# A two-layer decoder on one core: the first layer's pairs, its experts and the preparation of the second layer's weights planned as one graph, constants loaded inside it, expert weights laid out contiguously

## The chip, the core and the metric

The kernel runs on one core of a Trainium2 chip, as one launch of one program. The metric is the device time of that program in microseconds (us). Times are medians over several runs. A profile is one further execution, recorded instruction by instruction. The engines are TensorE (PE, with its weight loads PEld), VectorE (DVE), ScalarE (ACT), GpSimd (POOL) and SyncE (SP). SP and ACT issue ordinary DMAs, POOL issues indirect ones.

## What is computed

The input `x` has 32 sequences of 100 tokens with 256 channels, and there is a context of 361 rows for each sequence. Everything is 32-bit float. Two post-norm layers run one after the other:

```
x = layernorm(x + L0_attn(x))        # 16 heads of 16, rotary, causal
x = layernorm(x + L0_xattn(x, ctx))  # 8 heads, strided context positions
x = layernorm(x + L0_ffn(x))         # 64 experts of width 176, best 6 for each token, at most 128 tokens
                                     # to an expert, and one shared expert of width 352
x = layernorm(x + L1_attn(x))        # linear attention
x = layernorm(x + L1_xattn(x, ctx))  # full softmax over 361 rows, gated output
x = layernorm(x + L1_ffn(x))         # weights rounded to -1, 0, 1, activations to 8 bits
```

What matters here: an expert cannot start until every token of every sequence has chosen its experts, because the list of an expert's tokens runs over all of them; and the second layer's feed-forward needs both of its weight matrices reduced to a mean absolute value and then rounded (the "ternary weights").

## The kernel before

The program has four stages, one after the other.

1. **Start** (L434 to L553). The three down-projections of the first attention (1 MB each) are loaded by SP and multiplied on PE with their up-projections (L439 to L456). Then SP loads all constants of the first layer (L457 to L479: `wc`, `wqx`, `wkx`, `wvx`, `wox`, biases, `ws13`, `ws2`, rotary tables, masks). ACT's queue meanwhile writes zeros into the six routing tables (L515), into the tail of `x_dram` and `y_dram[0]` and, in 26 DMAs of 128 KB, into all of `y_dram[1]` (L521), and then loads every constant of the second layer (L527 to L548).
2. **Pairs** (`pair`, L608). The sequences go through the first layer two at a time, 16 pairs. A pair loads `xT`, `x` and its context `cR` (736 KB, two buffers), projects, sends queries and keys through DRAM (`dd`) into padded tiles `qpad` and `kpad`, does two score passes with a maximum between them (`nmx`, `nmT`, written into `qpad` by small DMAs), sends the result through DRAM again (`odd`, `sgd`), then cross attention from `cR` (keys at L781, values at L849), routing on DVE, and 12 indirect DMAs on POOL that write each token and its weight into the routing tables (L966). The shared expert's result goes to `y_dram[0]` (L1004).
3. **Experts** (`slots` L1008, `expert` L1038). `slots` reads the six tables into `lists` (L1014), adds them up (L1018), turns the result (L1024) and makes the row numbers `sidx` (L1029 to L1033). Then for each of 64 experts: SP loads `w13` (352 KB, as 256 rows of 1408 bytes) and `w2e` (176 KB, as 176 rows of 1024 bytes); POOL gathers 128 rows of `x_dram` (`xe`, L1046); PE turns them (L1054), multiplies by `w13` (through `dense`, L384) and by `w2e` (L1084); ACT and DVE do the gate; POOL scatters the result with an add into one of two `y_dram` (L1090). The weights have 6 buffers each, `xe`, `xeT` and `he` 3, `ye` 4. `prepare` (L555) has the same graph with the lowest priority: it makes `wog` and `bog` for the second layer from `wout` and `wgateT`, and the ternary weights `w1q` and `w2q` out of 1 MB loads into `wf` (L584 to L604).
4. **Second layer** (`sequence`, L1123): 32 sequences, one at a time in the program but overlapped by the planner.

The order of the work inside stages 2, 3 and 4 is set by a planner, `Flow` (L89 to L235). Every operation is entered with its engine, a cost in us, a latency for DMAs, what it reads and writes, and a priority. `emit` (L174) then steps through a clock of its own and picks, engine by engine, the operation that could start first, and among those the one with the lowest priority times `step` less the longest chain behind it. Buffers are rings with a fixed order of use; an operation that has no free buffer waits. The planner knows no DMA bandwidth: a DMA has a fixed latency whatever else is under way. What it decides is a fixed order for each engine, and on the chip each engine runs its list in that order, waiting where an input is late. Stages 2 and 3 have a graph each (`step` 20 and 1.5), with a pool of SBUF buffers each (`wa`, `we`). In the built program the DMAs of SP and ACT take eight completion semaphores in turn, and a DMA is not issued before the one that last had its semaphore has landed.

Of the kernel before, what the change touches and what calls it, by code (L numbers as in the profile page):

```python
# [238 lines left out]
def tile_decoder(ctx: ExitStack, tc: tile.TileContext, d, out):  # L239
# [56 lines left out]
    class Kit:  # L296
# [7 lines left out]
        def op(self, eng, cost, fn, r=(), w=(), **k):  # L304
            return self.fl.op(eng, cost, fn, r, w, pri=self.pri, **k)
# [151 lines left out]
    wc0 = w2(cA, "wc")  # L457
    wqx, wkx, wvx, wox = (w2(cA, n) for n in ("wqx", "wkx", "wvx", "wox"))
    bqx, bkx, bvx = (col(cA, n) for n in ("bqx", "bkx", "bvx"))
    nc.vector.tensor_scalar(bqx, bqx, SC32, None, ALU.mult)  # L460
    box = brow(cA, "box", T)
    gwT, gb = w2(cA, "gwT"), brow(cA, "gate_b", T, E)
    ws13 = w2(cA, "ws13")
    ws2 = cA.tile([128, 3, D], F32, name="ws2")
    nc.vector.memset(ws2[96:128, 2, :], 0.0)
    nc.sync.dma_start(ws2[:, 0:2, :], d["ws2T"][0:256].rearrange("(i p) n -> p i n", p=128))
    nc.sync.dma_start(ws2[0:96, 2, :], d["ws2T"][256:SI])

    nc.vector.tensor_scalar(ws2, ws2, 0.5, None, ALU.mult)
    rot0 = [table(cA, n) for n in ("cose", "sine", "coso", "sino")]  # L470
    pairmask, spread2 = table(cA, "pairmask"), table(cA, "spread2")
    causal = [table(cA, n) for n in ("causal", "causalT")]
# [3 lines left out]
    for i, t in enumerate(causal):  # L476
        mb = cA.tile([T, 4, T], BF16, name=f"mask{i}")
        nc.vector.tensor_copy(mb, t.unsqueeze(1).broadcast_to([T, 4, T]))
        masks.append(mb.rearrange("p r t -> p (r t)"))  # L479


    bvl_ = cA.tile([128, KC, T], F32, name="bvl_")
    for k in range(KC):
        nc.vector.tensor_scalar(bvl_[:, k, :], ones[:, 0:T], bvx[:, k : k + 1], None, ALU.mult)
    p = bank("pb")
    dense(p[0:T, 0:D], bvl_, wox)
    nc.vector.tensor_tensor(box, p[0:T, 0:D], box, ALU.add)
# [32 lines left out]
    for i in range((NTOK + CAP) // 128):  # L520
        nc.scalar.dma_start(y_dram[1][i * 128 : (i + 1) * 128, :], zero)  # L521
# [4 lines left out]
    q2 = nc.scalar  # L526
    wqkl, wvl, wol = (w2(cB, n, q2) for n in ("wqkT", "wvT", "woT"))  # L527
    bqkl, bvl, bol = brow(cB, "bqk", T, 2 * D, q2), brow(cB, "bv", T, D, q2), brow(cB, "bo", T, D, q2)
    headmask, spread = table(cB, "headmask", q2), table(cB, "spread", q2)
    wq1, wk1, wv1 = (w2(cB, n, q2) for n in ("wq1", "wk1", "wv1"))  # L530
    gam, bet = col(cB, "gamma", q2), col(cB, "beta", q2)
    cosq1, sinq1, cosk1, sink1, ebias = (
        table(cB, n, q2) for n in ("cosq1", "sinq1", "cosk1", "sink1", "ebias"))
    n1w, n2w = brow(cB, "norm1_w", T, D, q2), brow(cB, "norm2_w", T, HID, q2)
    asc, abi = brow(cB, "act_scale", T, 1, q2), brow(cB, "act_bias", T, 1, q2)
# [7 lines left out]
    q2.dma_start(wog[:, :, 0:D], d["woutT"].rearrange("(k p) n -> p k n", p=128))  # L543
    bog = cB.tile([T, 2 * D], F32, name="bog")
    for o, nm in enumerate(("bout", "bgate")):
        q2.dma_start(
            bog[:, o * D : (o + 1) * D],
            d[nm].rearrange("(o n) -> o n", o=1).broadcast_to([T, D]))  # L548

# [5 lines left out]
    def prepare(k):  # L555

        wraw, wg = k.V("wraw", [128, KC, D], 1), k.V("wg", [128, KC, D], 1)
        bcol, bl = k.V("bcol", [128, KC], 1), k.V("bl", [128, KC, T], 1)
# [12 lines left out]
        for m in range(KC):  # L571
# [8 lines left out]
            bog[:, D : 2 * D], bog[:, D : 2 * D], p[0:T, 0:D], ALU.add), r=[p])  # L580
        n = KC * HID
        for i, (nm, dst, nk) in enumerate((("w1fT", w1q, KC), ("w2fT", w2q, HID // 128))):
            wf, s, p = k.V("wf", [128, n], 1), k.V("ws", [128, 2]), k.P1()
            k.op("SP", 0.3, lambda wf=wf, nm=nm, nk=nk: nc.sync.dma_start(  # L584
                wf.t.rearrange("p (k n) -> p k n", k=nk),
                d[nm].rearrange("(k p) n -> p k n", p=128)), w=[wf], lat=6.0)
            k.op("DVE", 2.3, lambda wf=wf, s=s: nc.vector.tensor_reduce(
                s[:, 0:1], wf.t, AX.X, ALU.add, apply_absolute_value=True), r=[wf], w=[s])
            k.op("PE", 0.3, lambda s=s, p=p: nc.tensor.matmul(
                p[:, 0:1], lhsT=ones, rhs=s[:, 0:1], start=True, stop=True), r=[s], w=[p])  # L590

            def scales(s=s, p=p, i=i):
                nc.vector.tensor_scalar(
                    s[:, 0:1], p[:, 0:1], 1.0 / (128 * n), 1e-5, ALU.mult, ALU.max)
                nc.vector.reciprocal(s[:, 1:2], s[:, 0:1])
                nc.vector.tensor_scalar(
                    wscale[:, i : i + 1], s[:, 0:1], 1.0 / 127.0, None, ALU.mult)

# [8 lines left out]

    def pair(k, u):  # L608

        op, V, P1, P4 = k.op, k.V, k.P1, k.P4  # L610
        bs = range(GB)
        bT = lambda b: slice(b * T, (b + 1) * T)
        Xs = [V("x", [T, D], 8) for b in bs]
# [483 lines left out]
    with phase0:  # L1097
# [11 lines left out]
        for ref in [tk, tb, xd] + yd:  # L1109
            ref.touch = []  # L1110
# [608 lines left out]
```

## Time and profile before

| what | value |
|---|---|
| median of 3 runs | 2353.12 us (2348.57 to 2373.64) |
| the profiled execution's own time | 2301.36 us |
| its span, first to last instruction | 2299.6 us |
| mean granted TensorE clock in it | 0.873 |
| PE, DVE, POOL, ACT busy | 83%, 61%, 59%, 44% of the span |
| moved by DMA | 176.47 MB, mean 77 GB/s |

By the timeline the four stages lie so in the span: the first instruction of the first pair on PE starts at 51.5 us, the last table write of the last pair on POOL at 849.2 us, the first multiplication of an expert at 883.4 us, the last scatter of an expert at 1130.65 us, and the second layer runs from there to 2299.6 us.

How to read what follows: a line of the "stages" view gives a stretch in us, its length, then for each engine the busy us and the number of instructions, the clock that was granted to TensorE, the mean busy share of the 16 DMA engines and the GB/s. A line of the timeline gives start and length in us, engine and source line, output and inputs, and in brackets how long the engine had been idle and what ended that. Matmuls of 32-bit data appear as two or more instructions.

### The profile page before, as it was taken

What the parts mean: (1) busy time and instruction counts of PE and PEld (TensorE: products, weight loads), DVE (VectorE), ACT (ScalarE), POOL (GpSimd) and SP (SyncE); (2) the same over time, 40 slices, a digit from 0 to 9 for tenths busy, and PEclk for the clock granted to TensorE, in tenths of its full rate; (3) what the DMA queues carried; (4) which work ended last, traced back from release to release, by engine and by line L of the source; (5) the groups of instructions that cost most, each with busy time, mean ns of one, the idle gap of its engine ahead of it and who ended that gap; (6) DMA issues with size and microseconds to landing.
All of it is one profiled execution on the core that took longest, in us unless ns stands there. A gap on an engine that the chain in (4) does not pass through costs nothing.

```text
span 2299.6 us, 49312 instructions
## 1 busy us (share of the span) xinstructions
PE 1907.6 (83%) x18998; PEld 1409.0 (61%) x18998; DVE 1409.9 (61%) x3083; ACT 1018.2 (44%) x2001; POOL 1350.2 (59%) x1588
## 2 busy tenths in 40 slices
PE   4788988889988736888798889798999999999784
PEld 4666776777766525777565556565565655665452
DVE  1255446555454624222397788878888988888733
ACT  0232232332232201222254667466777777776554
POOL 0015334544443444666656777668888888887653
PEclk9788788987797857999898999889999999999765
DMA  8423333333422117888631222122222222221110
GB/s 253 130 55 62 65 65 49 63 70 58 63 48 50 20 34 196 211 209 214 136 80 35 61 55 51 48 57 51 60 56 64 55 63 62 57 59 36 33 23 10
DMA packets 196805, 176.47 MB, mean 77 GB/s; under 512 B 68625, under 2 KB 185331, under 8 KB 196571
## 3 DMA queue, kind: packets, MB, share of 16 engines
q1 hardware_dynamic: 169304, 148.34, 26.4%
q0 software_dynamic: 18432, 17.00, 4.4%
q10 hardware_dynamic: 8834, 7.99, 1.1%
q8 instruction: 150, 2.46, 0.5%
q14 instruction: 85, 0.69, 0.1%
HBM read 121.71 MB, written 51.06 MB: 75 GB/s over the span
## 4 chain that ended last, share of the span: by engine, by line
PE 28%; DVE 15%; issue 3%; ACT 2%; POOL 1%; DMA 1%; SPq 0%; DVEq 0%; POOLq 0%; ACTq 0%
PE banks L384 4%; PE banks L1387 4%; PE banks L1185 3%; PE banks L390 3%; DVE nmx L1394 3%; PE banks L1221 3%; DVE gt L1463 2%; PE banks L1408 2%; PE banks L376 2%; DVE X L1465 1%; PE banks L1554 1%; PE banks L1272 1%; PE banks L1360 1%; PE banks L1528 1%; DVE X L1238 1%
## 5 line engine op out<-in xcount | busy, mean ns | idle before, releaser
L1422 POOL TENSOR_TENSOR P<-P,ebias 121x800 f32<-121x800 f32 (+1 forms) x192 | 358.5, 1890 | 84.8 <-ACT P L1416 84.7
L966 POOL DMA_INDIRECT tab<-tw,tix x192 | 193.7, 1009 | 99.4 <-issue 52.3
L1394 DVE TENSOR_REDUCE nmx<-banks 100x4 f32<-100x1444 f32 x128 | 211.7, 1656 | 43.2 <-PE banks L1387 39.3
L1416 ACT ACTIVATE P<-banks 121x800 f32<-121x800 f32 (+1 forms) x192 | 150.1, 835 | 69.6 <-PE banks L1408 68.6
L390 PE MATMUL banks<-P,vpad 121*32 121x100 f32 (+2 forms) x4096 | 129.6, 273 | 22.1 <-DVE X L1338 16.5
L1387 PE MATMUL banks<-kpad,qpad 16*100 16x361 f32 x1024 | 124.9, 543 | 26.7 <-DVE nmx L1394 25.1
L390 PEld LDWEIGHTS banks<-P,vpad 121*32 121x32 f32 (+2 forms) x4096 | 98.7, 119 | 66.7 <-issue 24.1
L1090 POOL DMA_INDIRECT y<-ye,sidx x64 | 103.1, 1610 | 60.7 <-ACT ye L1088 37.8
L384 PE MATMUL banks<-xeT,w 128*88 128x128 f32 x1024 | 132.7, 290 | 0.3 <-DVE xeT L1060 0.3
L384 PEld LDWEIGHTS banks<-xeT,w 128*88 128x88 f32 x1024 | 128.7, 171 | 4.9 <-issue 0.6
L1408 PEld LDWEIGHTS banks<-qpad,kpad 17*121 17x121 f32 (+1 forms) x3072 | 96.1, 191 | 50.5 <-DVE nmx L1394 16.6
L1408 PE MATMUL banks<-qpad,kpad 17*121 17x100 f32 (+1 forms) x3072 | 112.3, 286 | 11.5 <-DVE nmx L1394 11.4
L337 POOL TENSOR_TENSOR rs<-rs,mhalf 100x1 f32<-100x1 f32 (+1 forms) x128 | 77.6, 606 | 52.9 <-DVE rs L351 41.6
L1074 DVE SCALAR_TENSOR_TENSOR he<-he,banks 88x256 f32<-88x256 f32 x64 | 26.7, 417 | 129.4 <-ACT he L1071 129.3
L1221 PE MATMUL banks<-wv,cT 128*121 128x256 f32 (+1 forms) x384 | 97.5, 392 | 4.3 <-ACT aoT L1334 4.3
L1185 PE MATMUL banks<-cT,wk 128*128 128x361 f32 x256 | 98.1, 510 | 0.0
L1046 POOL DMA_INDIRECT xe<-x_dram,sidx x64 | 64.6, 1009 | 53.7 <-PE banks L1054 23.0
L647 POOL TENSOR_TENSOR e<-e,tmp 128x200 f32<-128x200 f32 x32 | 19.0, 609 | 129.4 <-DVE tmp L645 76.2
L689 DVE TENSOR_REDUCE nmx<-banks 100x16 f32<-100x1600 f32 x32 | 58.1, 1819 | 50.5 <-PE banks L681 50.4
L1387 PEld LDWEIGHTS banks<-kpad,qpad 16*100 16x100 f32 x1024 | 38.9, 172 | 76.6 <-DVE nmx L1394 30.3
L384 PE MATMUL banks<-x,ws 128*128 128x200 f32 (+1 forms) x384 | 78.8, 356 | 3.8 <-DVE x L732 2.4
L1545 POOL TENSOR_TENSOR hn<-h,norm_w_bc 100x1024 f32<-100x1024 f32 x32 | 75.6, 2364 | 8.5 <-ACT h L1538 8.5
(300 smaller groups left out, 5035.9 us busy)
## 6 DMA issues: line engine op xcount, KB each, us to landing
w<-in_w13T SPq DMA_DIRECT2D x64, 352.0 KB
cR<-in_ctxR SPq DMA_DIRECT2D x16, 736.0 KB
kd<-kc SPq DMA_DIRECT2D x32, 361.0 KB
kpad<-kd SPq DMA_DIRECT2D x128, 90.2 KB
w2e<-in_w2T SPq DMA_DIRECT2D x64, 176.0 KB
cx<-in_ctx SPq DMA_DIRECT2D x32, 242.0 KB
odd<-pos SPq DMA_DIRECT2D x256, 25.0 KB
qpad<-nmT SPq DMA_DIRECT2D x256, 1.6 KB
```

The lines of the kernel that those rows point to most:

```text
L337: self.op("POOL", 0.4 + 0.16 * n, lambda: nc.gpsimd.tensor_tensor(r[:, 0:n], r[:, 0:n], mhalf[0 : r.t.shape[0], 0:n], ALU.pow), w=[r])
L384: nc.tensor.matmul(dst, lhsT=lhs[:, k, :], rhs=w[:, k, :], start=(k == 0), stop=(k == n - 1))
L390: nc.tensor.matmul(po[32 * j : 32 * j + 32, r * T : (r + 1) * T], lhsT=vs[:, 4 * r + j, :], rhs=Ps[j // 2][0 : vs.shape[0], j % 2, r, :], ...
L966: op("POOL", 1.3, lambda b=b, kk=kk: nc.gpsimd.indirect_dma_start(out=tables[kk], out_offset=bass.IndirectOffsetOnAxis(ap=tix[:, b, kk : k ...
L1090: op("POOL", 1.7, lambda: nc.gpsimd.indirect_dma_start(out=y_dram[e % 2], out_offset=bass.IndirectOffsetOnAxis(ap=sidx[:, e : e + 1], axis=0),
L1185: nc.tensor.matmul(p[:, 0:S], lhsT=wk1[:, k, o * 128 : (o + 1) * 128], rhs=cT[:, k, :], start=(k == 0), stop=(k == KC - 1),)
L1221: nc.tensor.matmul(p[0 : CHW[c], (c - c0) * D : (c - c0 + 1) * D], lhsT=cT[:, k, c * CH : c * CH + CHW[c]], rhs=wv1[:, k, :], start=(k == ...
L1387: nc.tensor.matmul(p[0:T, j, 0:S], lhsT=qpad[rg, r, :], rhs=kpad[rg, r, :], start=True, stop=True,)
L1394: op("DVE", 1.66, lambda r=r, p=p: nc.vector.tensor_reduce(nmx[:, 4 * r : 4 * r + 4], p[0:T, :, 0:S], AX.X, ALU.max, negate=True), r=[p], ...
L1408: nc.tensor.matmul(st[0:cw, j, r * T : (r + 1) * T], lhsT=kpad[rg, r, c * CH : c * CH + cw], rhs=qpad[rg, r, :], start=True, stop=True,)
L1416: op("ACT", 0.85, lambda cw=cw, half=half, st=st, P=P: nc.scalar.activation(P[0:cw].rearrange("p j r t -> p j (r t)"), st[0:cw, 2 * half : ...
L1422: nc.gpsimd.tensor_tensor(o, o, ebias[0:cw, c, :].unsqueeze(1).broadcast_to([cw, 8, T]), ALU.mult)
```

## The change

The change has four parts.

- **One graph.** Pairs and experts are entered into one `Flow` with `step` 20 and one SBUF pool. An expert's buffers are now those of the pairs: `w13` takes the ring `P` (4 buffers instead of 6), `w2e` the rings `pT` and `hT` in turn (2 each), `xe` the ring `x` (8 instead of 3), `xeT`, `he` and `ye` two rings of 2 each. `slots` reads the tables into the tiles `oh` and `prod` of the pairs and adds in two steps.
- **Constants inside the graph.** All constants of the first layer except the down-projections, the rotary tables and the causal masks, and all of the second layer, are now SP operations of the graph, sorted by the stage that needs them first ("a", "x", "r", "s", "1"). Operations that use them wait for the stage's loads. The 26 zero writes of `y_dram[1]` are one SP DMA of 3328 KB. ACT's queue keeps the 8 other zero writes.
- **Ternary weights between pairs.** `prepare` is cut into nine steps, entered after pairs 1 to 9. Each matrix is loaded twice, in halves of 512 KB, into the ring `cR`: once for the mean, once for the rounding.
- **Contiguous expert weights.** The host lays `w13T` out as [64, 128, 704] and `w2T` as [64, 88, 512], so that a partition's row is one piece of 2816 or 2048 bytes.

```diff
+    later = {"a": [], "x": [], "r": [], "s": [], "1": []}
+
+    def defer(stage, pool, key, shape, src):
+        t = pool.tile(shape, F32, tag=key, name=key)
+        later[stage].append(lambda: nc.sync.dma_start(t, src))
+        return t
...
+    spread2, wc0 = dtable("a", cA, "spread2"), d2("a", cA, "wc")
+    wqx, wkx, wvx, wox = (d2("x", cA, n) for n in ("wqx", "wkx", "wvx", "wox"))
...
-    for i in range((NTOK + CAP) // 128):
-        nc.scalar.dma_start(y_dram[1][i * 128 : (i + 1) * 128, :], zero)
...
-    q2 = nc.scalar
-    wqkl, wvl, wol = (w2(cB, n, q2) for n in ("wqkT", "wvT", "woT"))
...
+    wk1, wv1 = (d2("1", cB, n) for n in ("wk1", "wv1"))
...
+    def constants(k):
+
+        refs = {s: Ref(None, None) for s in later}
+        for s, fs in later.items():
+            for i, f in enumerate(fs):
+                k.op("SP", 0.3, f, w=[(refs[s], i)], lat=3.0, pri=2 if s == "1" else 0)
...
+        k.op("SP", 0.3, lambda: nc.sync.dma_start(
+            y_dram[1].rearrange("(a p) n -> p a n", p=128),
+            zero.unsqueeze(1).broadcast_to([128, (NTOK + CAP) // 128, D])), w=[yd[1]], lat=12.0,
+            pri=3)
+        return refs
...
+    def prepare(k, step):
...
+        if step < 8:
+            i, j = PIECES[step % 4]
...
+            wf = k.V("cR", [128, 1024])
+            k.op("SP", 0.3, lambda: nc.sync.dma_start(
+                wf.t.rearrange("p (k n) -> p k n", k=h),
+                d[nm].rearrange("(k p) n -> p k n", p=128)[:, j * h : (j + 1) * h, :]),
+                w=[wf], lat=4.0)
+            if step < 4:
+                k.op("DVE", 1.2, lambda: nc.vector.tensor_reduce(
...
-        w13, w2e = V("w13", [128, KC, 2 * IM], NW), V("w2e", [IC, 2, D], NW)
+        other = e % 2
+        w13, w2e = V("P", [128, KC, 2 * IM], 4), V(("pT", "hT")[other], [IC, 2, D])
         op("SP", 0.3, lambda: nc.sync.dma_start(
-            w13.t, d["w13T"][e].rearrange("(k p) n -> p k n", p=128)), w=[w13], lat=4.0)
+            w13.t, d["w13T"][e].rearrange("p (k n) -> p k n", k=KC)), w=[w13], lat=4.0)
...
-        xe = V("xe", [CAP, D], 3)
+        xe = V("x", [CAP, D], 8)
...
             k = Kit(wa, ps, 20.0)
+            k.refs = constants(k)
             for u in range(NG):
                 k.pri = u
                 pair(k, u)
-            k.fl.emit()
-        for ref in [tk, tb, xd] + yd:
-            ref.touch = []
-        with tc.tile_pool(name="we", bufs=2) as we, tc.tile_pool(
-            name="psle", bufs=1, space=PSUM) as ps, tc.manual_schedule():
-            k = Kit(we, ps, 1.5)
+                if 1 <= u <= 9:
+                    prepare(k, u - 1)
+            k.pri = NG
             sidx, sw = slots(k)
             for e in range(E):
-                k.pri = 1 + e
+                k.pri = NG + 0.15 * e
                 expert(k, e, sidx, sw)
-            k.pri = 500
-            prepare(k)
             k.fl.emit()
```

The order in which the built program issues its instructions can be listed without running it. In the second layer it is the same on every engine as before. In the changed first layer SP's list begins with the three down-projections, the rotary tables and masks, `spread2`, the first two `xT`, then `wc`, `x`, the four cross-attention weights, biases, the first `cR`; after the first pair's `dd` writes come the 3328 KB zero write, `wk1`, `wv1`, the second pair's first `dd` write, `gamma`, `beta` and `cosk1`, and only then the first pair's `qpad` and `kpad` loads; nearly all other constants of the second layer, the second pair's `qpad` and `kpad` loads and the first half of `w1f` stand before the first `qpad` write of `nmT`. On POOL, 11 gathers stand before the first scatter (8 before the change). On SP, the first four `w13` loads stand among the last pair's `odd` writes.

## Prediction before the result

> **What bounds the kernel now.** I read the stages view first, since the four stages have different limits.
>
> ```profile
> core 0: us, PE busy (x) PEld busy (x) DVE busy (x) ACT busy (x) POOL busy (x), PEclk, DMA share, GB/s
> 0.00:20.00 20.00, 10.85 (x51) 10.88 (x52) 2.92 (x23) 0.00 (x0) 4.18 (x16) 1.00 0.85 257
> 20.00:40.00 20.00, 11.99 (x51) 10.74 (x50) 2.52 (x11) 0.00 (x0) 0.00 (x0) 1.00 0.80 243
> 40.00:60.00 20.00, 5.62 (x16) 5.17 (x16) 2.39 (x7) 0.00 (x0) 1.17 (x2) 1.00 0.85 255
> 150.00:720.00 570.00, 504.61 (x5504) 410.44 (x5503) 313.12 (x723) 168.75 (x366) 253.19 (x330) 0.84 0.32 60
> 840.00:860.00 20.00, 0.00 (x0) 0.00 (x0) 0.82 (x1) 0.00 (x0) 7.90 (x8) 0.50 0.16 39
> 860.00:880.00 20.00, 3.43 (x9) 2.76 (x10) 4.02 (x9) 0.00 (x0) 2.90 (x3) 0.50 0.81 242
> 900.00:1120.00 220.00, 184.21 (x1258) 167.90 (x1257) 64.61 (x150) 58.49 (x144) 147.27 (x113) 0.91 0.85 206
> 1140.00:2299.00 1159.00, 1009.80 (x10400) 658.63 (x10400) 919.98 (x1946) 737.97 (x1376) 854.60 (x1024) 0.91 0.21 52
> ```
>
> The start is bound by DMA (share 0.80 to 0.85, about 250 GB/s). The pairs are bound by PE (504.6 of 570 us) with DMA at 0.32. From 840 to 880 PE does almost nothing. The experts run at a DMA share of 0.85 with PE at 184 of 220 us. The second layer takes half the time and the change doesn't touch it: its order is the same, so I leave it at its 1165 us. Next, the timeline at the two seams.
>
> ```profile
> 51.49 5.17 PEld L384 LDWEIGHTS banks<-xT,wqk 128*128 128x128 f32 x16 [16.04 <-DVE mask L478]
> 63.10 1.28 ACT L637 ACT_TABLE_LOAD   x1 [63.10 <-DMA x<-in_x]
> 86.45 2.31 SPq L416 DMA_DIRECT2D qpad<-nmT  x4
> 849.17 0.99 POOL L966 DMA_INDIRECT tab<-tw,tix  x1 [0.30 <-issue]
> 853.40 3.72 SPq L1014 DMA_DIRECT2D lists<-tab  x6
> 859.18 2.73 DVE L1018 TENSOR_REDUCE slot<-lists 64x256 f32<-64x1536 f32 x1 [24.64 <-DMA w2e<-in_w2T]
> 864.51 1.00 POOL L1046 DMA_INDIRECT xe<-x_dram,sidx  x1 [14.35 <-DMA w<-in_w13T]
> 864.61 0.39 SPq L584 DMA_DIRECT2D wf<-in_w1fT  x1
> 882.29 0.94 PE L1054 MATMUL banks<-ident,xe 128*128 128x128 f32 x4
> ```
>
> The first pair starts at 51.5 us, and ACT's first computation waits until 63.1, because its queue has been issuing DMAs. At the other seam the first gather (864.5) is used only at 882: it shares the DMA engines with six experts' weights (6 x 528 KB) and `prepare`'s loads (1 MB, 256 KB, 256 KB), issued together. Last, the waits of the expert stage and its two POOL operations by shape.
>
> ```profile
> PE banks L1054 <- DMA xe<-x_dram,sidx: 33.7, 16, 4.2
> L1090 POOL DMA_INDIRECT y<-ye,sidx x57 | 92.1, 1615 | 54.2 <-ACT ye L1088 34.9 <-issue 10.4 <-ACT he L1071 6.7
> L1046 POOL DMA_INDIRECT xe<-x_dram,sidx x56 | 55.2, 986 | 21.1 <-issue 11.9 <-PE banks L1054 6.0 <-DMA y<-ye,sidx 1.7
> ```
>
> PE's idle time here is nearly all one wait, for gathered rows (33.7 of 35.8 us); it never waits for weights. Gathers run at most three ahead (`xe` has 3 buffers).
>
> **Start: -4 us (-20 to 0).** Without ACT's traffic the 1 MB loads come sooner; three products (L445, 7.01 us each by the timeline) end near 27 us. `xT` cannot be loaded before that: in the built program its load waits for the third product, whose input lies in the same memory. So the first projection moves from 51.5 to about 30, and `s` follows at once instead of at 64. If this lead of 21 us were carried through, it would be the gain. But the planner, knowing no bandwidth, put the bytes ahead of the first pair's next steps. From 27 us, in SP's order before the first scores: 2931 KB to the `dd` write, 2892 KB to the next, the 3328 KB zero write, 894 KB, 400 KB of `qpad` and `kpad`: 10.7 MB, at 250 GB/s 43 us, so scores at 70 (before: 77.4). From there to the `qpad` write of `nmT` another 4.35 MB, 17 us: 87 us, before 86.45. At the rate of a full share (255/0.85 = 300 GB/s) it is 27 + 36 + 14.5 = 78, a gain of 9. I take 4. Here a rule speaks against the change: the Trainium skill ("DMA: Bandwidth & Descriptors", section "Issuing engines are not separate DMA queues") says that DMAs of all issuing engines run on the same 16 DMA engines and that a second issuer saves only issue time. The rows agree on the cause (0.85 share with two issuers), so moving ACT's loads to SP removes no byte from the road; the rule gives about 0 to -9, the timeline's 51.5 alone would give -21. I go with the rule. The kpad load also waits for the zero write's semaphore, and SP's whole list waits behind it; that is in the sum.
>
> **Pairs: +8 us (0 to +30).** `prepare` moves here. PE: the products for `wog` and `bog` took 3.75 + 1.91 us and two sums 0.3 each at the gap's low clock (0.50), about 3 us at a full one; PE is the bound, so +3. DVE: two reductions of 2.28, six passes of 1.2 to 1.3, copies of 0.42: 13.3 us, on an engine that is 55% busy, mostly hidden, +2; uncovered it would be +13. DMA: 8 loads of 512 KB and two of 256 KB at 0.32 share, hidden. The weights take `cR`'s ring in turn, so pairs 1 to 10 share one `cR` buffer: each next `cR` load waits on SP until the values (L849) of the pair before are through, and `dd`, `qpad` and `odd` DMAs of other pairs stand behind it. Before, SP had three such waits of 20.2 us in all; the keys that need the load come most of a pair (44 us) later. I take +3, between 0 and the three-fold of that wait, 60/3. `ws2`, `bqx` and `box` work (about 2 us) is only moved into a wait.
>
> **End of the pairs: +2 us (0 to +5).** Four `w13` loads (1408 KB, 5 us at 300 GB/s) stand among the last pair's `odd` and `sg` DMAs; most lies under their 2 us latencies.
>
> **Gap: -16 us (-18 to -10).** The chain last table write, tables, two adds (0.96 and 1.45 us by like rows, for 2.73), `sidx` stays; but the DMA engines are idle when the gathers are issued, because four experts' weights are in and `prepare` is gone. Gather at 864, rows after 2 to 3 us instead of 17.5: first turn at 866 instead of 882.
>
> **Experts: -21 us (-40 to 0).** From the first scatter (893.0) to the last (1130.65) 63 take 237.65 us; the last ones, with no loads left, run every 2.62 us, those between 900 and 1120 every 3.9. New parts: (a) `xe` 8 deep with 11 gathers up front, which removes the waits of 33.7 us or gives them to the next bound; (b) longer packets. By the trace's packet records an undisturbed 1408-byte packet takes 60 ns, one of 2816 112; 1024 takes 46, 2048 84. Per expert 256 x 60 + 176 x 46 = 23.5 engine-us become 128 x 112 + 88 x 84 = 21.7: 0.11 us of 16 engines, 7 us in 64. The same page (section "Why small descriptors are slow") puts a fixed 3 cycles on each packet, 47 against 44 for 1408 bytes: 3 to 4%, 0.05 us, 3 us in all. The trace's rows are nearer, I take them. The next bounds: POOL 0.99 + 1.61 + 2 x 0.30 = 3.2 us an expert; DMA 0.85 x 3.9 = 3.3, less 0.11, 3.2; PE 184/57 = 3.2. With three bounds at 3.2 none is reached: I take 3.55 for 55 experts and 2.62 for 8, 216 us for 237.65. If DMA at 0.85 is already full, it stays (0); at 3.2 it is -40. `w13` and `w2e` have 4 buffers for 6: 3 x 3.55 = 10.7 us ahead, against a few us for a load.
>
> **Sum:** -4 + 8 + 2 - 16 - 21 = -31 us. Against the profiled execution, 2301.36 (span 2299.6 and 1.8 around it), 2270. The median of the runs, 2353.12, stands 2.2% above that execution; scaled, -32: **2321 us**, -1.4%.
>
> **Rivals.** (1) *The lead is carried.* The start keeps its 21 us because DMA runs at 300 GB/s and the rest fits under PE, and the experts reach 3.2: -21 + 3 - 16 - 40 = -74, about 2279. For it: PE's order in the first pairs is almost unchanged and nothing else is late. Against: 15 MB before the first `nmT` write. Chance 0.20. (2) *The bytes decide everywhere.* Start 0, experts stay at 3.9 because a 0.85 mean share is full: 0 + 8 + 2 - 16 - 3 = -9, about 2344. For it: the 0.85; against: from 920 to 940 us the stages view has 0.97 and 235 GB/s. This is also the case that the change doesn't do what it says. Chance 0.21. (3) *Slower: SP's list blocks.* With one `cR` buffer, SP stands at nine loads until the values before are done. The price is what PE loses each time; if each of the nine costs PE over 4 us (the three waits before averaged 6.7 us of SP), it eats the 32 us gained elsewhere; at 6.7 it is 60 - 3 - 32 = +25, about 2378. For it: planner clock and chip drift apart where PE is granted 0.84. Against: SP waits for PE when PE is the one behind. Chance 0.12. The forecast has 0.47, its own range 2300 to 2342.
>
> **How the numbers follow.** A change of about 1% (23.5 us, 2329.6) is what a measurement of this kernel can tell from none. Faster: 0.36 of the forecast's 0.47, all of (1), 0.02 of (2): 0.58. Within 1%: 0.11 + 0.19 = 0.30. Slower: 0.12. The range leaves out most of (3) and the far end of (1): 2268 to 2358.
>
> **What would show it.** First projection near 30 us, but the first `qpad` write of `nmT` still at 75 to 88. The last table write at 849 + 6, give or take 10. First expert turn 15 to 18 us after it (before 33). PE's waits for gathered rows under 10 us in all, DMA share above 0.9, scatters every 3.5 us. The second layer 1165 us as before. Wrong would be: SP waits for values that PE then idles on, a weights wait in the experts, or a second layer that is longer.

## The result, and the profile after

The changed kernel takes 2341.60 us (median of 20 runs, 2332.89 to 2354.89), the kernel before 2359.39 us in the same set (20 runs, 2340.53 to 2376.96): a ratio of 0.9932 [0.9908, 0.9957], or 16 us less. The forecast was 2321 us, 32 less. The profiled execution of the changed kernel (2337.44 us) lies inside its runs; that of the kernel before (2301.36 us) lies below all 20 of its own. So the pairs of the two first traces can't be subtracted, and both kernels were traced again on one chip (below). The ratios leave disturbed executions out, so a ratio isn't always the quotient of the two medians.

First the stages view of the changed kernel's first trace, with the columns of the earlier one: PE, weight loads, DVE, ACT and POOL busy, granted clock, DMA share, GB/s.

```profile
40.00:60.00 20.00, 9.61 (x85) 7.73 (x83) 2.76 (x7) 1.45 (x4) 1.17 (x2) 0.74 1.02 319
150.00:720.00 570.00, 452.49 (x4692) 361.55 (x4692) 277.44 (x633) 141.49 (x306) 217.51 (x283) 0.81 0.29 62
950.00:970.00 20.00, 16.63 (x96) 15.56 (x97) 4.61 (x11) 3.60 (x9) 13.75 (x14) 0.75 0.63 162
985.00:1160.00 175.00, 157.68 (x1134) 143.28 (x1133) 52.89 (x129) 51.54 (x128) 126.60 (x98) 0.96 0.93 234
```

Between 40 and 60 us the DMA engines are full (1.02, 319 GB/s): the deferred bytes fall just there. From 150 to 720 us PE has 452 us of work where the first trace of before had 505, but these are the two executions that can't be subtracted. At the second seam PE is busy again from 950 us, and the experts run at a DMA share of 0.93 with PE at 158 of 175 us. The same seams in the timeline:

```profile
28.27 1.28 ACT L695 ACT_TABLE_LOAD   x1 [28.27 <-DVE wv L449]
30.38 4.91 PE L384 MATMUL banks<-xT,wqk 128*128 128x200 f32 x14 [2.64 <-DMA xT<-in_xT]
85.15 2.29 SPq L416 DMA_DIRECT2D qpad<-nmT  x4
...
935.77 0.99 POOL L1024 DMA_INDIRECT tab<-tw,tix  x1 [0.30 <-issue]
947.41 1.00 POOL L1110 DMA_INDIRECT x<-x_dram,sidx  x1 [10.66 <-DVE sidx L1096]
950.23 0.66 PE L1118 MATMUL banks<-ident,x 128*128 128x128 f32 x2 [3.94 <-DMA x<-x_dram,sidx]
```

The first projection starts at 30.4 us (before 51.5), but the first row maxima are written at 85.15 (before 86.45). The first gathered rows are used 14.5 us after the last table write (before 33.1), 2.8 us after their gather. PE's two longest waits in the expert stage:

```profile
PE banks L1118 <- ACT od L1152: 13.0, 6, 2.7
PE banks L1118 <- DMA x<-x_dram,sidx: 4.4, 2, 3.9
```

The wait for gathered rows is gone (4.4 us for 33.7). A smaller one has come, for ACT (13.0 us): the turn (L1118) of the gathered rows waits for a PSUM bank, a piece of PE's output memory, that ACT empties into `od` (L1152). 63 scatters take 211.9 us for 237.65.

### The profile page after: what moved, and what is told of

Read it like the earlier page. It is cut to its first block, busy times and chain, and to the rows that moved or that the text cites. A ratio compares the mean times of both kernels' runs of the same rounds, so it can differ in the third digit from the quotient of the medians.

```text
span 2335.7 us, 49255 instructions
## 1 busy us (share of the span) xinstructions
PE 1918.1 (82%) x18998; PEld 1408.3 (60%) x18998; DVE 1408.9 (60%) x3093; ACT 1019.5 (44%) x2001; POOL 1347.0 (58%) x1589
## 4 chain that ended last, share of the span: by engine, by line
PE 26%; DVE 15%; issue 3%; ACT 2%; POOL 2%; DMA 2%; SPq 1%; DVEq 0%; POOLq 0%; ACTq 0%
PE banks L384 4%; PE banks L1445 3%; PE banks L1243 3%; PE banks L390 3%; DVE nmx L1452 2%; DVE gt L1521 2%; PE banks L1279 2%; PE banks L1466 2%; PE banks L376 2%; DVE X L1523 1%; PE banks L1418 1%; PE banks L1612 1%; PE banks L1330 1%; DVE X L1296 1%; PE banks L1586 1%
## 5 line engine op out<-in xcount | busy, mean ns | idle before, releaser
L1445 PE MATMUL banks<-kpad,qpad 16*100 16x361 f32 x1024 | 123.0, 534 | 25.4 <-DVE nmx L1452 23.8
L756 ACT ACTIVATE P<-banks 100x800 f32<-100x800 f32 x64 | 50.8, 834 | 96.4 <-PE banks L739 64.7
L384 PE MATMUL banks<-x,ws 128*128 128x200 f32 (+1 forms) x384 | 86.7, 381 | 0.6 <-issue 0.4
L384 PE MATMUL banks<-xT,wqk 128*128 128x200 f32 x256 | 59.3, 387 | 28.0 <-DMA xT<-in_xT 14.4
L1110 POOL DMA_INDIRECT x<-x_dram,sidx x64 | 62.7, 979 | 31.8 <-issue 13.1
L1550 ACT ACTIVATE hn<-hn,magic,mx 100x256 f32<-100x256 f32 x64 | 58.6, 915 | 46.2 <-DVE mx L1546 31.3
L384 PEld LDWEIGHTS banks<-x,ws 128*128 128x128 f32 (+1 forms) x384 | 75.0, 210 | 6.1 <-issue 2.0
```

The costliest lines, as they stand in the source:

```text
L384: nc.tensor.matmul(dst, lhsT=lhs[:, k, :], rhs=w[:, k, :], start=(k == 0), stop=(k == n - 1))
L1445: nc.tensor.matmul(p[0:T, j, 0:S], lhsT=qpad[rg, r, :], rhs=kpad[rg, r, :], start=True, stop=True,)
```

## The experiments

The kernel before took 2256 to 2278 us on five chips and 2359 in the first set, so each kernel is set against the kernel before on its own chip. The kernels of one group, between rows of dashes, ran on one chip. A difference of two ratios, given below in us, has an interval of some 8 to 15 us to either side. The last column is the last table write in the kernel's own trace, the end of the pairs.

| kernel | us | before | ratio [95%] | pairs end, us |
|---|---|---|---|---|
| before_again | 2269.55 (one run) | 2256.07 | | 827.55 |
| after_again | 2246.47 (one run) | 2256.07 | | 857.64 |
| own_ring | 2248.70 | 2256.07 | 0.9975 [0.9951, 0.9999] | 844.61 |
| prep_last | 2223.50 | 2256.07 | 0.9849 [0.9804, 0.9895] | 829.92 |
| --- | | | | |
| after_timed | 2273.14 | 2267.91 | 1.0006 [0.9981, 1.0032] | 867.56 |
| prep_loads | 2249.10 | 2267.91 | 0.9916 [0.9890, 0.9943] | 843.43 |
| prep_shift | 2274.68 | 2267.91 | 1.0040 [1.0019, 1.0062] | 873.75 |
| late_bytes | 2239.66 | 2267.91 | 0.9868 [0.9819, 0.9917] | 848.30 |
| --- | | | | |
| prep_lat | 2255.45 | 2269.84 | 0.9938 [0.9915, 0.9961] | 857.95 |
| late_zero | 2269.45 | 2269.84 | 0.9993 [0.9964, 1.0022] | 868.22 |
| before_contig | 2269.21 | 2269.84 | 0.9989 [0.9960, 1.0019] | 831.72 |
| late_last | 2223.18 | 2269.84 | 0.9785 [0.9743, 0.9827] | 812.75 |
| --- | | | | |
| after_third | 2272.42 | 2270.37 | 1.0018 [0.9996, 1.0039] | 864.84 |
| own_lat | 2258.76 | 2270.37 | 0.9959 [0.9934, 0.9983] | 856.05 |
| late_lat | 2236.74 | 2270.37 | 0.9869 [0.9822, 0.9916] | 838.38 |
| before_xe8 | 2251.92 | 2270.37 | 0.9930 [0.9899, 0.9961] | 834.40 |
| --- | | | | |
| own_pri | 2231.33 | 2278.10 | 0.9797 [0.9756, 0.9837] | 831.42 |
| late_pri | 2214.81 | 2278.10 | 0.9732 [0.9693, 0.9772] | 807.22 |

### Both kernels again, on one chip

No edit: `before_again` and `after_again`, and later the changed kernel timed on two more chips.

> The kernel before, unchanged, for a second trace. Theory A (the change lengthens the pairs: 936 us to the last table write after the change, 849 before): the last table write is again near 849 us and the whole again near 2300. Theory B (the first trace of before was an unusually quick execution, below all the runs that were timed): the last table write comes near 890 to 910, the whole near 2350, and the second layer is still about 1165.

> The changed kernel, unchanged, for a second trace on the same chip as before_again. Both theories: last table write near 936, experts 212 us from the first to the last scatter, second layer 1161. If the pairs differ here by over 30 us from the first trace, their length is a matter of the execution (the granted clock, or the time that instructions take to arrive) and single traces of this stage can't be set against each other.

> The changed kernel, unchanged, timed beside the three that follow on one chip, since chips differ by some 4%. In the second pair of traces (one chip) the pairs ended 30 us later than before (857.6 for 827.6 us), and gap and experts took 233 us for 271. Theory A (prepare between the pairs takes back most of the gain): 0.990 to 0.997 of the kernel before. Theory B (the pairs lose nothing that lasts): 0.983 to 0.987.

> The changed kernel, unchanged, a third time, as the base of the three beside it. If the chip decides (before takes 2256 to 2270 us here and 2359 where the change stood at 0.993): 0.998 to 1.003 again on a chip that runs before in 2250 to 2275. If it scatters from set to set whatever the chip: anywhere from 0.992 to 1.002.

The timeline's last table write, first and last scatter, of before_again:

```profile
827.55 0.99 POOL L966 DMA_INDIRECT tab<-tw,tix  x1 [0.30 <-issue]
870.69 1.64 POOL L1090 DMA_INDIRECT y<-ye,sidx  x1 [0.30 <-issue]
1098.76 1.55 POOL L1090 DMA_INDIRECT y<-ye,sidx  x1 [0.30 <-issue]
```

and of after_again:

```profile
857.64 0.98 POOL L1024 DMA_INDIRECT tab<-tw,tix  x1 [0.30 <-issue]
883.09 1.64 POOL L1154 DMA_INDIRECT y<-od,sidx  x1 [0.30 <-issue]
1090.63 1.55 POOL L1154 DMA_INDIRECT y<-yT,sidx  x1 [0.54 <-issue]
```

To the end of the pairs the change loses 30.1 us. From there to the first scatter it gains 17.7 (43.1 to 25.4), and from the first to the last 20.5 (228.1 to 207.5). The rest of the span, the second layer, is 1169.0 and 1154.1 us here, but 1168.2 and 1168.1 in after_timed and after_third: the same instructions in the same order, so the 14 us are no effect of the change. 30 lost against 38 gained is nearly nothing, and the timed runs on two chips say just that: 1.0006 and 1.0018. Theory B falls; theory A, that the pairs take the gain back, holds, and more fully than its 0.990 to 0.997. after_again's pairs end 78 us before those of the first trace (935.77), so by what was expected of it single traces from different chips can't be set against each other. The 30.1 us don't rest on one pair of traces, though: on another chip after_third ends its pairs 30.4 us behind before_xe8 (864.84 and 834.40), whose pairs are those of the kernel before. The first set's 0.9932 lies outside both later intervals; before took 2359 us there, 2256 to 2278 later.

### What of prepare costs: own_ring, prep_loads, prep_shift, prep_last

```diff
 own_ring:
-            wf = k.V("cR", [128, 1024])
+            wf = k.V("wf", [128, 1024], 1)
-        bcol, bl = k.V("bcol", [128, KC], 1), k.V("xT", [128, KC, T])
+        bcol, bl = k.V("bcol", [128, KC], 1), k.V("bl", [128, KC, T], 1)
 prep_loads: the three ternary tiles are set to zero, and after the load of a piece
+            if step < 8:
+                return
 prep_shift:
-                if 1 <= u <= 9:
-                    prepare(k, u - 1)
+                if 3 <= u <= 11:
+                    prepare(k, u - 3)
 prep_last: those two lines left out, and after the loop over the experts
+            for step in range(9):
+                k.pri = NG + 30
+                prepare(k, step)
```

> The ternary weights' pieces get a buffer of their own and the bias product one too, so the pairs have both cR buffers again. Theory A, in the form of the prediction's third rival (SP's list blocks on the single cR buffer): 20 to 60 us below the changed kernel, near 2300. Theory B (nothing is lost in the pairs): within 8 us of the changed kernel, 2334 to 2350.

> Of prepare's first eight steps only the loads stay (same buffers, same queue); reductions, scales and passes on VectorE and the two small sums on TensorE are left out, so the ternary weights are zeros. Theory A1 (the loads and the shared cR buffer are what costs): as slow as the changed kernel, within 6 us, about 0.993 of before. Theory A2 (the VectorE passes, some 13 us, stand in the pairs' chain softmax to TensorE): 12 to 30 us quicker, 0.981 to 0.988. Theory A3 (any operation added between the pairs only reshuffles the planner's order, and the order is what costs): anything from 0.983 to 1.000.

> The same nine steps, entered after pairs 3 to 11 instead of 1 to 9; same work, another order. Theories A1 and A2 (a fixed price of the work or of the buffer): within 6 us of the changed kernel. Theory A3 (the order decides): off by more than 8 us, either way.

> The nine prepare steps are entered after the experts with the lowest priority, so the pairs are free of them; the rest of the change stays. Theory A (any part of prepare between the pairs costs: buffer, DVE or PE): the last table write comes 30 to 80 us earlier than in the changed kernel, and what comes back at the end of the experts is about 10 to 25 us (13 us of DVE and 4.5 MB of loads), so 2290 to 2330. Theory B: the last table write does not move by more than 10 us, and the whole is 0 to 15 us longer than the changed kernel, 2340 to 2357.

own_ring is not the answer: 0.9975, some 7 us below the changed kernel's 1.0006 on another chip, where 20 to 60 were expected. prep_shift decides nothing: by the ratios it lies 7.7 us above the changed kernel on the same chip (1.5 by the medians), between the 6 us of theories A1 and A2 and the 8 of A3. prep_loads leaves the reductions and passes out, so its ternary weights are zeros; its second layer takes 1167 us all the same (1168 in after_timed). It gives back 0.0090, or 20 us, so the VectorE passes, reductions and their small sums are a large part. prep_last gives everything back: its pairs end at 829.92, as before (827.55), and the gap and experts keep their gain. But by its trace nearly all of prepare is still between the pairs: the reductions ran from 708 to 760 us, the passes from 762 to 795, the products for `wog` from 784, because the planner found room there. The same 13 us of VectorE's work between the pairs, once costly and once free: it isn't the work, it's where it stands.

### Where it stands: prep_lat, own_lat, own_pri

The trace of after_timed says how one such place costs. VectorE's own waits from 60 to 870 us for the pieces' loads:

```profile
DVE wsum L612 <- DMA cR<-in_w1fT: 25.7, 2, 17.3
DVE cR L632 <- DMA cR<-in_w2fT: 8.7, 2, 7.5
```

and three of these places in its timeline:

```profile
83.13 1.22 DVE L612 TENSOR_REDUCE wsum<-cR 128x1 f32<-128x1024 f32 x1 [8.49 <-DMA cR<-in_w1fT]
84.54 0.36 DVE L703 TENSOR_TENSOR tmp<-banks,sine 128x200 f32<-128x200 f32 x1
85.49 0.83 PE L734 MATMUL banks<-mask,identb 100*100 100x400 bf16 x2 [5.92 <-DVE tmp L703]
...
95.68 0.49 SPq L607 DMA_DIRECT2D cR<-in_w1fT  x1
103.29 1.22 DVE L612 TENSOR_REDUCE wsum<-cR 128x1 f32<-128x1024 f32 x1 [17.26 <-DMA cR<-in_w1fT]
104.43 3.55 DVE L747 TENSOR_REDUCE nmx<-banks 100x16 f32<-100x1600 f32 x2
106.30 0.25 PE L411 MATMUL banks<-ident,nmx 100*16 100x100 f32 x1 [2.68 <-DVE nmx L747]
...
423.06 0.53 SPq L607 DMA_DIRECT2D cR<-in_w2fT  x1
427.18 0.75 DVE L632 TENSOR_SCALAR cR<-cR,wsum 128x1024 f32<-128x1024 f32 x1 [7.53 <-DMA cR<-in_w2fT]
427.85 0.41 DVE L790 TENSOR_TENSOR x<-x,banks 100x256 f32<-100x256 f32 x1
428.31 1.56 PE L390 MATMUL banks<-P,vpad 100*32 100x100 f32 x32 [4.49 <-DVE x L790]
```

In each of the three a pair's operation on VectorE starts only after one of prepare's that waited for a load. At 427 us VectorE has stood 7.5 us at a prepare pass whose load SP issued only at 423.06; the residual add of a pair stands behind it, and PE behind that add (4.5 us). At 83 and 103 us it is the same, with 5.9 and 2.7 us of PE. PE's three waits are 13.1 us together. So prep_lat tells the planner that a load takes longer:

```diff
 prep_lat: the load of a piece
-                w=[wf], lat=4.0)
+                w=[wf], lat=24.0)
 own_lat: prep_lat and own_ring together
 own_pri: own_lat, with the nine steps entered after the experts as in prep_last
```

> One number is changed: the planner reckons 24 us instead of 4 from the issue of a prepare piece's load to its use, so that the VectorE passes are put later in VectorE's order; work, buffers and queue stay. Theory A2b (VectorE stands still in its order before these passes, 8.5 + 17.3 + 1.1 + 7.5 us by the changed kernel's trace, because the load behind them was issued late; the pairs' operations stand behind it and TensorE waits for them): VectorE's waits for these loads fall under 5 us, and the kernel is 8 to 25 us below the changed one, 0.990 to 0.997 of before where the changed kernel had 1.0006. Theory A1 (the buffer and SP's list): no change, 0.998 to 1.003. Theory A3 (the order as such): any value, with no relation to VectorE's waits.

> The later passes (24 us reckoned for a piece's load) and a buffer of their own for the pieces and the bias product. If what is left of the pairs' loss is the shared cR buffer: 8 to 20 us below the later passes alone (0.9938), 0.985 to 0.990. If the buffer costs nothing: 0.992 to 0.996.

> As own_lat (own buffers, 24 us reckoned for a piece's load), but the nine steps are entered after the experts with the lowest rank. By the built order the reductions still come early, beside pairs 1 to 3, and the passes beside the last three pairs. If the rank among the pairs' operations is what own_lat still loses: 0.983 to 0.988, as prep_last. If any prepare work beside the first pairs disturbs them, whatever its rank: 0.992 to 0.998.

In prep_lat VectorE's waits for pieces are gone from the waits view, and the kernel falls from 1.0006 to 0.9938: 15 us, about PE's 13.1. (The waits alone don't set the time, though: prep_shift has 11.4 us of them for 34.4 and is no quicker.) A new wait of PE has come in prep_lat, because the pieces now hold `cR` for longer, and a pair's context has to wait for it:

```profile
PE banks L839 <- DMA cR<-in_ctxR: 21.3, 4, 8.7
```

own_lat has none of this wait and, at 0.9959, still gains nothing on top. That is no clean test of the shared `cR` buffer, since the hole described next is longer there. But in the three later traces of the changed kernel PE never waits for a context load: there theory A1, the shared buffer as the cost, has nothing to point to. own_pri differs from own_lat only in the rank of the nine steps and in the place where they are entered, and stands at 0.9797, 37 us lower (each against before on its own chip) and below both ranges expected of it. Up to the tenth pair the two traces run alike (its `ww` at 581.08 and 580.60 us); the eleventh comes at 695 in own_lat and at 614 in own_pri, and the pairs end at 856 and 831. What lies there is the ninth step, which takes both `Vx` buffers for `wout` and `wgateT`, a sharing that I had left in place in own_ring and own_lat. The step's timeline in own_lat, with the pairs' own writes of `Vx` (L914):

```profile
478.39 0.42 SPq L642 DMA_DIRECT2D Vx<-in_wout  x1
485.71 0.62 DVE L914 TENSOR_TENSOR Vx<-banks,pairmask 92x512 f32<-92x512 f32 x1
553.63 0.46 SPq L642 DMA_DIRECT2D Vx<-in_wgateT  x1
647.39 1.03 PE L384 MATMUL banks<-Vx 128*128 128x256 f32 x4
658.16 0.69 DVE L914 TENSOR_TENSOR Vx<-banks,pairmask 92x512 f32<-92x512 f32 x1 [2.03 <-PE banks L907]
```

and the same in own_pri:

```profile
487.48 0.62 DVE L914 TENSOR_TENSOR Vx<-banks,pairmask 92x512 f32<-92x512 f32 x1
520.48 0.69 DVE L914 TENSOR_TENSOR Vx<-banks,pairmask 92x512 f32<-92x512 f32 x1 [2.77 <-PE banks L907]
...
744.85 0.67 DVE L914 TENSOR_TENSOR Vx<-banks,pairmask 92x512 f32<-92x512 f32 x1
746.00 0.38 SPq L642 DMA_DIRECT2D Vx<-in_wout  x1
```

From 486 to 658 us no pair of own_lat writes `Vx`: buffers are given out in the order of entry, the step entered between two pairs holds them, and its products, which nothing waits for, come late. A pair's second attention can't pass. In own_pri the step gets its buffers after the last pair. In after_timed the hole is shorter (485 to 555 us, the weights loaded at 531 and 547), but it is there: own_pri writes `Vx` 35 us sooner, at 520. What it does to the pairs can be read from the tenth and the twelfth `ww`, an operation of each pair's routing, in after_timed:

```profile
594.46 0.94 DVE L1009 TENSOR_REDUCE ww<-oh 100x12 f32<-100x768 f32 x1
704.88 0.95 DVE L1009 TENSOR_REDUCE ww<-oh 100x12 f32<-100x768 f32 x1
```

and in own_pri:

```profile
580.60 0.94 DVE L1009 TENSOR_REDUCE ww<-oh 100x12 f32<-100x768 f32 x1
644.86 0.95 DVE L1009 TENSOR_REDUCE ww<-oh 100x12 f32<-100x768 f32 x1
```

Between them lie 110 us in one and 64 in the other. The ten later traces in which the ninth step is entered after the tenth pair have 99 to 154 us there, the four in which it comes last 64 (the kernel before, with another order, 90); and in prep_shift, where it is entered after the twelfth pair, the twelfth to the fourteenth take 121 us for own_pri's 94. Part of this is made up later: from the tenth `ww` to the last table write after_timed takes 273 us, prep_loads 274, own_lat 275, own_pri 251. So in these three the ninth step costs 22 to 24 us at the end of the pairs (in own_ring, with 257, only 6). prep_loads loses as much without any pass, so the rank of the passes (602 to 743 us in own_lat, 756 to 849 in own_pri) isn't needed to explain it. That it is the hold on `Vx`, and not the step's rank, is argued from the hole: a kernel that changes the `Vx` sharing alone wasn't run. Some 12 of the 37 us don't show in the pairs at all; the interval is as wide.

### The start's bytes: late_bytes, late_zero

```diff
 late_bytes: stage "1" and the zero write are taken out of constants();
+    def late(k, u):
+        fs, gate = later["1"], [(xd, u * GB)]
+        for i in range(3 * u - 3, min(3 * u, len(fs))):
+            k.op("SP", 0.3, fs[i], r=gate, w=[(k.refs["1"], i)], lat=3.0)
+        if 9 <= u <= 10:
...
                 pair(k, u)
+                if 1 <= u <= 10:
+                    late(k, u)
 late_zero: the zero write alone goes late
```

> The second layer's constants go three a pair behind the x write of pairs 1 to 9, the 3.3 MB zero write in two halves at pairs 9 and 10; prepare stays. The prediction's reading (the start's lead of 21 us is lost to these bytes): the first write of the row maxima comes at 62 to 70 us instead of 85, and 10 to 20 us of it stay to the end: 8 to 20 us below the changed kernel. Rival (PE's work, not the first bytes, bounds the pairs, so a lead given at the start runs dry in the next stall, or the order changes with it): within 6 us of the changed kernel.

> Of the start's late bytes only the 3.3 MB zero write goes to pairs 9 and 10; the second layer's constants stay at the start. If the zero write alone holds the start up (it alone takes 7.1 us of SP at the next DMA, and 11 us of all the DMA engines): first write of the row maxima at 70 to 75 us instead of 86, and 8 to 15 us below the changed kernel, 0.993 to 0.997. If it is the number of bytes as a whole: half of what moving all gave (33 us), 0.990 to 0.995. If it is the issue times of the 25 constants on SP: under 5 us, 0.998 or more.

The stages view from 40 to 90 us, first after_timed, then late_bytes:

```profile
40.00:60.00 20.00, 9.08 (x84) 7.37 (x82) 2.72 (x7) 1.45 (x4) 1.17 (x2) 0.74 1.03 322
60.00:90.00 30.00, 14.27 (x146) 10.98 (x146) 6.55 (x8) 0.92 (x4) 1.17 (x2) 0.65 0.69 193
```

```profile
40.00:60.00 20.00, 11.56 (x120) 9.61 (x119) 2.91 (x8) 1.45 (x4) 1.17 (x2) 0.74 0.70 199
60.00:90.00 30.00, 23.41 (x333) 17.53 (x332) 11.13 (x11) 6.01 (x13) 1.17 (x2) 0.78 0.41 113
```

With the bytes gone, the DMA share falls from 1.03 to 0.70 and PE has 23.4 us of work between 60 and 90 instead of 14.3. The first write of the row maxima in late_bytes:

```profile
66.00 4.52 SPq L416 DMA_DIRECT2D qpad<-nmT  x8
```

That is 20 us before after_timed's 85.81, and the pairs end 19 us earlier (848.30 for 867.56). The ratio falls by 0.0138, 31 us, more than the lead; VectorE's waits for prepare's pieces, 34.4 us in after_timed, are 13.7 here. In late_zero the first maxima come at 75.73, half the lead, but the waits for pieces are as long as before (36.6 us) and nothing is left at the end (0.9993). So an early lead doesn't by itself reach the end; where both kernels are free of these waits, the late bytes are worth 16 us (late_lat against prep_lat) and 15 us (late_pri against own_pri, on one chip).

Are the bytes the cause, or the time that SP needs to issue them? late_zero's first maxima came close to what was expected of the zero write (70 to 75 us), its ratio is what was expected of the issues (0.998 or more). From 60 to 90 us the DMA share of after_timed is 0.69, and SP issues one DMA after another:

```profile
81.43 0.42 SPq L471 DMA_DIRECT2D wq<-in_wq  x1
81.90 0.47 SPq L471 DMA_DIRECT2D cosq<-in_cosq  x1
```

21 such constants between 58 and 86 us take 11.4 us of SP, and the issue right behind the zero write 7.1: together 18.5 of the 20 us. In the kernel before ACT issued all of these. So the second half of the lead goes to SP's list at least as much as to the bytes; a kernel with the same issues and fewer bytes wasn't run.

### The experts: before_contig, before_xe8

```diff
 before_contig: the contiguous layout of w13T and w2T and their two loads, in the kernel before
 before_xe8: the kernel before with
-        xe = V("xe", [CAP, D], 3)
+        xe = V("xe", [CAP, D], 8)
```

> The kernel before with contiguous expert weights alone. The experts' stage became 20.5 us shorter on one chip (228.1 to 207.5). If packets of twice the length are the cause: 10 to 20 us of it appear here, 0.991 to 0.996. If the deeper gathers (8 buffers for 3) are the cause, as the prediction had it: 3 to 7 us, 0.997 to 1.000, and TensorE still waits 25 us or more for gathered rows.

> The kernel before with 8 buffers for gathered rows instead of 3, nothing else. If the depth of the gathers is what shortened the experts' stage by 20 us, as the prediction had it: TensorE's waits for gathered rows fall from 31 to 36 us to under 10, the stage from the first to the last scatter from 228 to about 210, and the kernel stands at 0.991 to 0.994. If the depth only shows the next limit (the weights' loads, or the loads of prepare that share the road): 0.996 to 1.000, and a wait of PE for weights or for other engines takes its place.

The contiguous weights alone give 0.9989 [0.9960, 1.0019]: 2.5 us, not to be told from none. The gathers' depth alone gives 0.9930, 16 us. PE's waits in the experts of before_again:

```profile
PE banks L1054 <- DMA xe<-x_dram,sidx: 29.3, 17, 3.9
```

and of before_xe8:

```profile
PE banks L1054 <- ACT ye L1088: 20.6, 17, 4.1
```

The wait for rows vanishes, and two thirds of it come back as a wait for ACT; from first to last scatter the stage takes 215 us for 228. The changed kernel has 207.5: the other 7.5 us aren't explained, since before_contig doesn't show them and an expert stage without prepare's loads wasn't run by itself.

### Together: late_last, late_lat, late_pri

late_last is late_bytes with prep_last, late_lat late_bytes with prep_lat, late_pri late_bytes with own_pri.

> Both corrections in one: prepare entered after the experts, the second layer's constants and the zero write among pairs 1 to 10. Alone they gave 0.985 and 0.987 of before (on two chips). If the two losses are separate, the start's 20 us and the pairs' 25 to 35 us add up: 0.970 to 0.978. If the late bytes merely gave cover for prepare, or the two share one loss: 0.982 to 0.988.

> The late bytes (constants and zero write at pairs 1 to 10) and the later passes together, prepare still between the pairs. If the two losses are separate (33 and 15 us): 0.978 to 0.982. If the late bytes had already removed most of VectorE's standing still (its waits for pieces were 13.7 us there for 34.4): 0.983 to 0.988.

> The late bytes, and prepare as in own_pri. Best version so far: 0.9785 (late bytes and prepare last, on the shared buffer). If the buffer and the waits for pieces (10 us of VectorE there) still cost: 0.972 to 0.977. If not: 0.977 to 0.984.

late_lat adds nothing to late_bytes (0.9869 for 0.9868): the late bytes had already removed most of VectorE's standing still. late_last adds 19 us, late_pri some 12 more, as expected if the shared buffer and the waits for pieces still cost, but the two intervals don't tell it from none: 0.9732 [0.9693, 0.9772] is the best version, 2.7% below the kernel before, with the pairs ending at 807.22 us.

## Why the prediction was wrong

**Start, -4: near in size, the cause half right.** First projection near 30 us (30.38), first row maxima at 75 to 88 (85.15); on one chip they moved by +0.7 us (86.04 for 85.37). late_bytes shows that the 20 us are real once the bytes are elsewhere. The section of the Trainium skill that the prediction quotes ("DMA: Bandwidth & Descriptors", "Issuing engines are not separate DMA queues") says that a second issuer saves only the time of issuing, and the prediction put that time at nothing. While the DMA share is 1.02 the bytes do eat the lead; after that, at 0.69, the issues that SP took over from ACT are as good a cause (11.4 us). In the pairs that follow even the -4 is not seen: after_again's first pair reaches its routing at 179.15 us, before_again's at 170.66.

**Pairs, +8: the step that failed.** With start and tail the sum to the last table write was +6; on one chip it was +30.1, of which the start has +0.7. So pairs and tail, put at +10, came to some +29, near the far end of the range. Of the three terms for the pairs, the buffer on SP (+3, between 0 and 60/3) is about nothing: PE never waits for a context load in the later traces of the changed kernel, and SP's waits at the pairs' `cR` loads are 19 us in after_timed for 21 in before_again. With it goes the mechanism of the third rival. The failed term is VectorE's: "13.3 us, on an engine that is 55% busy, mostly hidden, +2; uncovered it would be +13." A mean busy share says nothing of a list that is run in order: the passes wait for loads, and what stands behind them waits too. It measured 15 us (prep_lat) to 20 (prep_loads). And one term was not in the sum at all: the ninth step between the pairs, which takes both `Vx` buffers and costs 22 to 24 us at the end of the pairs. I had followed `cR`, one of three rings that the diff shares out, and not the other two. With both mended the pairs end as they did before the change (831.42 in own_pri, 827.55 to 834.40 in the three later traces with the pairs of the kernel before).

**End of the pairs, +2,** can't be seen apart from the pairs.

**Gap, -16: right.** -17.7 on one chip; the first turn came 14.5 us after the last table write, just under the 15 to 18 that were said.

**Experts, -21: right in size, for the right reason.** -20.5. Waits for rows 4.4 us (under 10), DMA share 0.93 (over 0.9), a scatter every 3.36 us (3.5). The depth of the gathers carries most of it (16 us in before_xe8's time, 13 in its stage); some 7 us of the stage stay unexplained. Of the two parts the packets were given 7 us from the trace's rows, where the page's fixed cost made an estimate of 3; before_contig shows 2.5, with an interval of 7 us to either side, so neither is shown nor excluded.

**Second layer:** 1154 to 1172 us from trace to trace, in both kernels alike: unchanged.

So the mechanisms of both gains were right, and the loss up to the end of the pairs was put at a fifth of what it was. What stays open: why the first set of runs has 0.9932 and the two later ratios, on two chips, 1.0006 and 1.0018; whether the ninth step costs by its hold on `Vx` or by its rank; and how the start's lead divides between bytes and issues.

## What to carry to other kernels

Where an engine runs a fixed list, as here, work that is moved between the operations of a bounded stage should not stand in the list before its data have come, and should not hold a buffer of theirs that is given out in order; giving it the lowest rank, behind everything else, did both at once here (own_pri, late_pri). Price it by what stands behind it, not by its duration and the engine's idle share. A phase that starts earlier is worth only what is kept out of its way, in bytes and in issues: defer loads by their use, not to the first moment at which a queue is free. Judge a profiled execution by where it lies among the timed runs before sums are made on it.

## What the runs showed of the hardware

The kernel before has medians of 2256 to 2278 us on five chips, and 2359 in the first set. Within one chip longer runs tend to have a lower mean granted clock: after_third's quickest run had 2260.56 us at 0.884, its longest 2287.85 at 0.872. And an issue that takes 0.60 us in late_zero, where the zero write comes later, kept SP for 7.10 us right behind the 3.3 MB zero write, in the timeline of after_timed:

```profile
48.21 0.59 SPq L589 DMA_DIRECT2D y<-zero  x1
48.85 7.10 SPq L471 DMA_DIRECT2D wk<-in_wk  x1
```
